# The seam between an expert loop and a linear attention: how partial sums reach one array in DRAM

## The chip, the cores and the metric

The kernel runs on one core of one Trainium2 chip. The metric is device microseconds (us) from the start to the end of one execution; lower is better. All data are float32.

The engines are named as in the profile: PE (matrix products), PEld (the loading of its weights), DVE (vector), ACT (activations), POOL (a second vector engine, which also starts indirect transfers), SP (which starts most transfers). `SPq`, `POOLq` and the like are an engine's own sequencer, which issues transfers (DMAs).

## The reference

The input has 4096 rows of 256 numbers. Four layers follow, each of the same form:

```
x = x + LN(attention(LN(x)))      # 16 heads, windows of 64 rows
x = x + LN(experts(LN(x)))        # 8 experts, each row goes to the best 2, plus a shared expert
x = x + LN(linear_attn(LN(x)))    # 16 heads, cos/sin position factors, causal, gated
x = x + LN(recurrence(LN(x)))     # forget/input/candidate gates over steps, then tanh
```

The change lies at the end of the second layer and the start of the third. The second layer is, for a row `x` (after its LN),

```
y  = sum over its 2 experts e of  weight_e * (silu(x @ w1[e]) * (x @ w3[e])) @ w2[e]     # hidden 704
y += (silu(x @ sw1) * (x @ sw3)) @ sw2                                                    # hidden 384
```

so each row of the result is a sum of three parts: two of chosen experts, one of the shared expert. The third layer needs the whole sum of a row before its LN. Its first operations are the LN of `y`, the addition to `x`, another LN, a transpose, and the products with `Wq` and `Wk`.

## The kernel before

**Units and blocks.** The 4096 rows are 32 tiles of 128 rows, or 16 *units* of 256 rows (0 to 15). For the experts, rows are sorted by expert into *blocks*: 32 large ones of 256 rows (two tiles, `nt = 2`) and 4 small ones of 128 rows (one tile). More small blocks stand in a branch (`tc.If`, L1303) that this input does not take.

**First layer (up to some 400 us).** It is written in an order fixed by hand (`ORDER_A`, `TAIL_A`), and its end sends every row to its two blocks by indirect scatters on POOL (L816), with a `memset` of the tiny tile `apart` between two of them (L964). The shared expert of units 0 to 11 is computed here (`NSA = 12`) and written to the DRAM array `ysh_d` (`shared_store`, L645); the rows of units 13 to 15 (`NSD = 13`) are set to zero (L706).

**The expert loop (400 to 890 us).** It goes over the list `line` (L1247 to 1251): the large blocks in order, and a small one after blocks 7, 15, 23 and 31. One step of the loop (for a block i)

- starts the weights of block i + 1 (`load_up`, L234 to 244, `load_down`, L246 to 260; SP),
- computes `up` of block i: in five parts of the hidden layer, each with its products (L1173), SiLU on ACT (L1178) and a product on DVE (L1180), and a rest of 64 columns,
- loads the rows of block i + 2 (`x_rows`, SP) and transposes those of block i + 1 (`x_cols`, PE and ACT),
- does one piece of a table of angles (`angle_piece`, L1071 on; DVE and ACT) and
- `down` of block i - 1: products (L1218, L1225), then for each tile a multiplication by the row's weight into a tile `yo` (DVE, L1228), and an indirect transfer that *adds* this tile to the rows of `ysh_d` (POOL, L1229).

Nobody knows at build time which rows an add touches, so the framework takes all adds to `ysh_d` as touching the same memory: each one waits until the one before it has landed. The tiles `yo` are a ring of five buffers (`tag="yo", bufs=5`).

The shared expert of unit 12 is computed at the start of the loop (`shared_part`, L1098; `shared_out`, L1126) and written to `ysh_d`. Its sums go through the same ring, as tiles `sy`.

**The seam (890 to 955 us).** After the loop, `second_weights` (L993) starts the loads of the attention's weights (`wl1`, `wl2`; SP). Then the third layer begins as a stream of small pieces: `flow(items, ORDER_C)` gives them one by one, in the order of `ORDER_C` with a lag for each piece, and `until(name, item)` issues pieces up to the first one of that name. The items are the units in the order 0, 8, 1, 9, 2, 10 ... The first pieces of a unit are

- `fy` (L322): load the unit's 256 rows of `ysh_d` into a tile `k_y` (SP); these tiles are a ring of four in the pool `kb`, which lasts to the end of the third layer,
- `bo_st`, `bo_pw`, `bo_nr`, `bo_ap` (L285 to 315): LN of `k_y` (statistics and shift on DVE, the power on POOL, the application on ACT),
- `bo_ad` (L335): add to `x` on POOL,
- `cn_st` ... `cn_ap`: the next LN, written back into `k_y`,
- `xt` (L1372, PE: four transposes `c_xt`), `xc` (L1385, ACT: copy to `c_xT`), `qk0`, `qk1` (L1391, PE: four products `c_pqk` each).

Between the pieces of units 0 and 8, PE is given the shared expert of units 13 to 15 (`shared(i, c)`, i = 0 to 2; L1322). Parts c = 0 to 2 are the three thirds of the hidden layer (`spg`: products, SiLU, product `sh` on DVE). Part 3 is the sums (`spd`: 3 products for each of two tiles; the profile shows every product as two PE instructions), copied by DVE into two tiles `sy` of the `yo` ring (L1122) and then *added* to `ysh_d` by two transfers of 128 KB on POOL, since the experts' adds have been going to those rows as well:

```
until("bo_st");  shared(0, 0..3)
until("bo_nr");  shared(1, 0)
until("bo_ad");  shared(1, 1)
until("cn_pw");  shared(1, 2);  shared(1, 3)
until("xt");     shared(2, 0..3)
```

Right behind it the loop's pools are closed, and 8 loads of 256 KB (2 MB) for the recurrence of the fourth layer are started on SP (L1354 to 1360) into the buffers of the last expert weights (`wl3`, `wl4`). The pools of the third layer (`c_sb` first, L1363) then take over the memory of the closed ones, and each new tile waits for whoever still uses that memory.

**The rest (955 to 1403 us).** The third layer continues in the order of `ORDER_C`, and the fourth layer's first steps are threaded into its end (`until("ps0", 9 + i)` and so on, L1689 on).

Of the kernel before, what the change touches and what calls it, by code (L numbers as in the profile page):

```python
# [9 lines left out]
F32 = mybir.dt.float32  # L10
I32 = mybir.dt.int32
AF = mybir.ActivationFunctionType
ALU = mybir.AluOpType
# [3 lines left out]
P = 128  # L17
D = 256
# [22 lines left out]
NSD = 13  # L41
# [99 lines left out]
def kernel(  # L141
# [7 lines left out]
    nc = tc.nc  # L149

    const = ctx.enter_context(tc.tile_pool(name="const", bufs=1))
# [114 lines left out]
    ysh_d = dram.tile([(NT + 1) * P, D], F32, name="ysh_d")  # L266
# [88 lines left out]
    row0 = const.tile([P, NB], I32, name="row0")  # L355

    key = const.tile([P, NB], F32, name="rt_key")
    n_small = const.tile([P, 1], I32, name="n_small")


# [2 lines left out]
    with ExitStack() as ph:  # L363
        wp = ph.enter_context(tc.tile_pool(name="a_w", bufs=1, side="right"))
# [253 lines left out]
        H = {}  # L618
# [62 lines left out]
        seen = pconst("rt_seen", [P, E])  # L681

        zero = wp.tile([P, XW], F32, name="zero")
        apart = wp.tile([P, 1], F32, name="apart")

        def later_constants():
            for f in range(4):
# [280 lines left out]
        with tc.manual_schedule(  # L968
# [14 lines left out]
            for it in TAIL_A:  # L983
                name, u = it.split(".")
# [8 lines left out]
    def second_weights():  # L993
# [27 lines left out]
    kb = ctx.enter_context(tc.tile_pool(name="take", bufs=2, side="right"))  # L1021
# [4 lines left out]
        out=causal, in_=causal, compare_op=ALU.is_ge, fill=0.0, base=0,  # L1026
# [6 lines left out]
        out=diag, in_=diag, compare_op=ALU.is_ge, fill=0.0, base=0,  # L1033
# [3 lines left out]
        out=diag, in_=diag, compare_op=ALU.is_ge, fill=0.0, base=31,  # L1037
# [17 lines left out]
    with ExitStack() as ph:  # L1055
        yp = ph.enter_context(tc.tile_pool(name="b_y", bufs=1, side="right"))
        hp = ph.enter_context(tc.tile_pool(name="b_h", bufs=2, side="right"))
# [40 lines left out]
        def shared_part(u, c, H):  # L1098
            xt = xnT[u // 2][:, :, (u % 2) * 256 : (u % 2) * 256 + 256]
            if c < 3:  # L1100
                pg = ps_up.tile([P, 2, BS], F32, name=f"spg{u}_{c}", tag="up")
                for i in range(2):
                    col0 = i * SHID + c * P
                    for k in range(2):
                        nc.tensor.matmul(
                            pg[:, i, :], ws_up[:, k, col0 : col0 + P], xt[:, k, :],
                            start=(k == 0), stop=(k == 1),
                        )
                sg = hp.tile([P, BS], F32, name=f"ssg{u}_{c}", tag="sg", bufs=3)
                nc.scalar.activation(sg, pg[:, 0, :], AF.Silu)  # L1110
                h = hp.tile([P, BS], F32, name=f"sh{u}_{c}", tag="h", bufs=10)
                nc.vector.tensor_tensor(h, sg, pg[:, 1, :], ALU.mult)
                H[c] = h
                return
            for t in range(2):
                pd = ps_d.tile([P, 2, D], F32, name=f"spd{u}_{t}", tag="pd")[:, 0, :]
                for i in range(3):
                    nc.tensor.matmul(
                        pd, H[i][:, t * P : (t + 1) * P], ws_down[:, i, :],
                        start=(i == 0), stop=(i == 2),  # L1120
                    )
                y = hp.tile([P, D], F32, name=f"sy{u}_{t}", tag="yo", bufs=5)  # L1122
                nc.vector.tensor_copy(y, pd)
                H[3, t] = y

        def shared_out(u, H):  # L1126
            for t in range(2):
                r0 = (2 * u + t) * P
                rows = ysh_d[r0 : r0 + P, :]
                if u < NSD:  # L1130
                    nc.sync.dma_start(out=rows, in_=H[3, t])
                else:
                    nc.gpsimd.dma_start(out=rows, in_=H[3, t], accum_op=ALU.add)


        def row_of(b):
# [6 lines left out]
        def x_rows(b, nt, at=None):  # L1143
            at = row_of(b) if at is None else at
            xg = hp.tile([P, 2, XW], F32, name=f"xg{b}", tag="xg", bufs=5)
            got = nc.sync.dma_start(
                out=xg[:, 0:nt, :],
                in_=xg_d[bass.ds(at, nt * P), :].rearrange("(t p) d -> p t d", p=P),
            )
            for name in dispatched:  # L1150
                data_dep(got, name, "a block's rows come from any token")
            return xg
# [50 lines left out]
        def down(b, nt, wb, hs, xg):  # L1203

            ws = hp.tile([P, 3, 2], F32, name=f"rt_w{b}", tag="rt_w")
            for i, op in enumerate((ALU.is_equal, ALU.not_equal)):
                nc.vector.scalar_tensor_tensor(
                    ws[:, i, 0:nt], xg[:, 0:nt, D + 2], key[:, b : b + 1], xg[:, 0:nt, D + i],
                    op, ALU.mult,
                )  # L1210
            nc.vector.tensor_tensor(ws[:, 2, 0:nt], ws[:, 0, 0:nt], ws[:, 1, 0:nt], ALU.add)
            pds = [
                ps_d.tile([P, 2, D], F32, name=f"pd{b}_{t}", tag="pd")[:, 0, :]
                for t in range(nt)
            ]
            for t in range(nt):
                for c in range(5):
                    nc.tensor.matmul(  # L1218
                        pds[t], hs[c][:, t * P : (t + 1) * P], wb[:, c, :],
                        start=(c == 0), stop=False,  # L1220
                    )

            for t in range(nt):
                r = slice(64 * t, 64 * t + 64)
                nc.tensor.matmul(pds[t], hs[5][r, :], wb[r, 5, :], start=False, stop=True)  # L1225
            for t in range(nt):
                yo = hp.tile([P, D], F32, name=f"yo{b}_{t}", tag="yo", bufs=5)
                nc.vector.tensor_scalar(yo, pds[t], ws[:, 2, t : t + 1], None, ALU.mult)  # L1228
                nc.gpsimd.indirect_dma_start(  # L1229
                    out=ysh_d[:, :],  # L1230
                    out_offset=bass.IndirectOffsetOnAxis(
                        ap=xg[:, t, D + 3 : XW].bitcast(I32), axis=0
                    ),
                    in_=yo,
                    in_offset=None,
                    compute_op=ALU.add,
                )

        def expert_of(b):
            return nc.values_load(  # L1240
                owner[0:1, b : b + 1], engines=[mybir.EngineType.SP],
                min_val=0, max_val=E - 1,
                skip_runtime_bounds_check_because="clamped where it is computed",
            )
# [2 lines left out]
        line = []  # L1247
        for i in range(NL):
            line.append((i, 2))
            if i % 8 == 7:  # L1250
                line.append((NL + i // 8, 1))
        rows = [x_rows(*line[0], 0)]

        H = {}
        for c in range(4):
            shared_part(NSA, c, H)
            next(tables, None)
        for _ in tables:
            pass
        nc.sync.dma_start(  # L1260
            out=th, in_=th_d.rearrange("f i d -> (f i d)").partition_broadcast(P)
# [8 lines left out]
        for i in range(len(line)):  # L1270
# [19 lines left out]
            if i + 1 < len(line):  # L1290
                wbs.append(load_down(i + 1, ev))
            pending = (*line[i], wbs[i], hs, rows[i])
        down(*pending)

        ws_down = shared_down(1)
# [7 lines left out]
        with tc.If(used > NS_ALWAYS):  # L1303
            for b in range(NL + NS_ALWAYS, NB):
                ev = expert_of(b)
                wa, wb = load_up(b, ev, wa_s), load_down(b, ev, wb_s)
                xg = x_rows(b, 1)
                down(b, 1, wb, up(b, 1, wa, x_cols(b, 1, xg)), xg)
# [5 lines left out]
        def until(name, item=0):  # L1314

            while todo_next[0] != (name, item):
                todo_next[0] = next(todo)

        todo_next = [next(todo)]
        H = [{}, {}, {}]  # L1320

        def shared(i, c):  # L1322
            shared_part(NSD + i, c, H[i])
            if c == 3:
                shared_out(NSD + i, H[i])
# [2 lines left out]
        until("bo_st")  # L1328
        for c in range(4):
            shared(0, c)  # L1330
        until("bo_nr")
        shared(1, 0)
        until("bo_ad")
        shared(1, 1)
        until("cn_pw")
        shared(1, 2)
        shared(1, 3)
        until("xt")
        for c in range(4):
            shared(2, c)  # L1340

    xt_stack.close()
# [9 lines left out]
    w_x = [kview(fl[:, i * 512 : (i + 1) * 512], 2) for i in range(3)]  # L1352
    w_c = [kview(fl[:, i * 512 : (i + 1) * 512], 2) for i in (3, 4)]
    w_c.append(kview(fm[:, 0:512], 2))  # L1354
    w_ox = kview(fm[:, 512:1024], 2)
    w_oc = kview(fm[:, 1024:1536], 2)
    for dst, src in zip(
        w_x + w_c + [w_ox, w_oc], (wfT, wiT, wcT, ufT, uiT, ucT, woT, uoT)
    ):
        nc.sync.dma_start(out=dst, in_=src.rearrange("(k p) f -> p k f", p=P))  # L1360

    with ExitStack() as ph:
        cb = ph.enter_context(tc.tile_pool(name="c_sb", bufs=2))  # L1363
# [315 lines left out]
        def first_cell(p):  # L1679
            f, i, g, c = (spare(8 * p + j) for j in (4, 5, 6, 7))  # L1680
            nc.vector.tensor_tensor(i, i, g, ALU.mult)
            for m in range(2):
# [2 lines left out]
                    ALU.mult, ALU.add,  # L1685
                )


        for i, u in enumerate((0, 8, 1, 9)):  # L1689
            until("ps0", 9 + i)  # L1690
# [258 lines left out]
```

## Time and profile before

| | us |
|---|---|
| median of three runs | 1393.34 |
| the three runs | 1393.34, 1394.17, 1390.73 |
| the profiled execution, its own time | 1404.6 |
| its span in the profile | 1402.9 |

The profiled execution is one execution of its own, slower than the median by 11.3 us, and every duration below is from it. Engine-busy shares are averages over the whole span: PE 95%, DVE 62%, ACT 42%, POOL 40%. The transfers move 139 MB, most of it before 910 us.

A line of the timeline has a start, a duration, the engine, the line in the kernel, the operation, "out<-in" by the program's names, the shape, and the count of like operations that follow one another. In square brackets stands how long the engine had been idle before it and what released it. Releasers are inferred: an instruction that waits for several things is put down to the one that came last by the profile, and where the one named had long been done, it was another. A line of a window gives, for a stretch of time, the busy time of each engine and the number of its instructions, then the clock granted to PE (1.00 is full speed), the busy share of the DMA engines and the rate of the transfers in GB/s.

### The profile page before, as it was taken

How to read it: one execution, taken by the hardware profiler on the slowest of the kernel's cores; microseconds unless marked ns; L12 is line 12 of the kernel's file. 1: busy time of each engine (PE TensorE's matmuls, PEld its weight loads, DVE VectorE, ACT ScalarE, POOL GpSimd, SP SyncE). 2: the span in 40 equal slices, each digit the busy share in tenths (PEclk: the TensorE clock that was granted, in tenths of full speed). 3: DMA queues.
4: the chain of work that ended last, by engine and by line, in shares of the span. 5: the costliest groups of instructions: out<-in, count | busy, mean ns of one | idle time of the engine just before them, and what ended most of it. 6: DMA issues, size and time to landing. Idle time of an engine off the chain costs nothing. (4 is left out here: it accounts for less than half of the span.)

```text
span 1402.9 us, 29800 instructions
## 1 busy us (share of the span) xinstructions
PE 1330.3 (95%) x11456; PEld 1098.0 (78%) x11456; DVE 870.2 (62%) x2586; ACT 583.2 (42%) x1306; POOL 558.3 (40%) x677
## 2 busy tenths in 40 slices
PE   6999999998699999999999999869999999999996
PEld 5888888786588888888888888646777777788885
DVE  5879787787354555555455642237878897645434
ACT  4766666563122222222222222025665665435443
POOL 3535657655311221212212212234766675433333
PEclk9999999998899999999999999979999999999998
DMA  8000111115746675666658566740000000000001
GB/s 218 2 17 21 35 44 51 47 36 195 216 145 201 174 229 162 182 202 199 197 157 233 164 204 173 137 104 22 18 18 17 18 3 2 2 1 31 16 31 45
DMA packets 120481, 139.13 MB, mean 99 GB/s; under 512 B 26704, under 2 KB 99600, under 8 KB 120336
## 3 DMA queue, kind: packets, MB, share of 16 engines
q1 hardware_dynamic: 105792, 117.91, 26.6%
q0 software_dynamic: 13728, 18.23, 6.9%
q8 instruction: 92, 1.51, 0.4%
q10 hardware_dynamic: 816, 1.06, 0.2%
q14 instruction: 53, 0.43, 0.1%
HBM read 104.83 MB, written 32.33 MB: 98 GB/s over the span
## 5 line engine op out<-in xcount | busy, mean ns | idle before, releaser
L1173 PE MATMUL pg<-xgT,wa 128*128 128x256 f32 (+1 forms) x1440 | 305.5, 371 | 1.8 <-ACT xgT L1162 1.8
L1173 PEld LDWEIGHTS pg<-xgT,wa 128*128 128x128 f32 x1440 | 259.9, 191 | 45.8 <-issue 11.3
L1229 POOL DMA_INDIRECT ysh_d<-yo,xg x68 | 106.2, 1562 | 427.3 <-DVE yo L1228 211.7
L1178 ACT ACTIVATE sg<-pg 128x256 f32<-128x256 f32 (+1 forms) x180 | 66.9, 372 | 354.6 <-PE pg L1173 353.6
L1180 DVE TENSOR_TENSOR h<-sg,pg 128x256 f32<-128x256 f32 (+1 forms) x180 | 73.0, 406 | 204.3 <-ACT sg L1178 201.7
L1218 PE MATMUL pd<-wb,h 128*128 128x256 f32 x680 | 152.8, 379 | 0.0
L1218 PEld LDWEIGHTS pd<-wb,h 128*128 128x128 f32 x680 | 126.4, 190 | 16.0 <-issue 0.3
L523 POOL TENSOR_TENSOR a_pn<-a_p,a_ri 128x512 f32<-128x512 f32 x64 | 66.6, 1045 | 90.1 <-DVE a_ri L517 50.2
L1527 DVE TENSOR_TENSOR c_et<-c_pe,causal 128x512 f32<-128x512 f32 x128 | 83.2, 682 | 22.2 <-PE c_pe L1517 21.9
L816 POOL DMA_INDIRECT xg_d<-xrow,slot x64 | 64.8, 1012 | 23.0 <-issue 9.9
L632 PE MATMUL a_sh<-xnT,was 128*128 128x256 f32 x288 | 73.4, 401 | 0.0
L1391 PE MATMUL c_pqk<-wl,c_xT 128*128 128x512 f32 x128 | 63.8, 622 | 8.0 <-ACT c_xT L1385 7.9
L1781 PE MATMUL d_pg<-d_xT,wl 128*128 128x256 f32 x288 | 70.2, 379 | 0.0
L632 PEld LDWEIGHTS a_sh<-xnT,was 128*128 128x128 f32 x288 | 56.2, 199 | 8.8
L1781 PEld LDWEIGHTS d_pg<-d_xT,wl 128*128 128x128 f32 x288 | 54.6, 190 | 7.6 <-ACT d_gt L1787 0.2
L496 DVE TENSOR_REDUCE a_mx<-a_s 128x8 f32<-128x512 f32 x64 | 42.7, 683 | 16.7 <-PE a_s L486 16.1
L1461 POOL TENSOR_TENSOR c_kn<-c_sq,xrow 128x512 f32<-128x512 f32 x32 | 42.2, 1319 | 12.9 <-ACT c_sq L1404 12.9
L1391 PEld LDWEIGHTS c_pqk<-wl,c_xT 128*128 128x128 f32 x128 | 23.2, 193 | 27.0 <-issue 16.1
L502 DVE TENSOR_TENSOR a_p<-a_s,a_mx 128x512 f32<-128x512 f32 x64 | 43.2, 675 | 0.8
L510 ACT ACTIVATE a_p<-a_p 128x512 f32<-128x512 f32 x64 | 40.1, 629 | 7.3 <-DVE a_p L502 6.7
L515 DVE TENSOR_REDUCE a_sm<-a_p 128x8 f32<-128x512 f32 x64 | 43.1, 674 | 0.0
L1082 DVE SCALAR_TENSOR_TENSOR ang<-kk,ang 128x256 f32<-128x256 f32 x96 | 40.9, 426 | 3.3
(313 smaller groups left out, 2787.0 us busy)
## 6 DMA issues: line engine op xcount, KB each, us to landing
wa<-in_w_dram SPq DMA_DIRECT2D x36, 704.0 KB
wa<-in_w_dram SPq DMA_DIRECT2D x36, 640.0 KB
wb<-in_w_dram SPq DMA_DIRECT2D x36, 640.0 KB
xg<-xg_d SPq DMA_DIRECT2D x32, 260.0 KB
xg_d<-zero SPq DMA_DIRECT2D x8, 650.0 KB
wb<-in_w_dram SPq DMA_DIRECT2D x72, 64.0 KB
x<-in_x_dram SPq DMA_DIRECT2D x16, 256.0 KB
k_y<-ysh_d SPq DMA_DIRECT2D x16, 256.0 KB
```

Source lines behind the costliest of these rows:

```text
L502: nc.vector.tensor_tensor(pr, S[u]["s"][g], S[u].pop(("m", g)).unsqueeze(2).to_broadcast([P, 8, 64]), ALU.subtract,)
L523: nc.gpsimd.tensor_tensor(to, S[u].pop(("p", g)), S[u].pop(("ri", g)).unsqueeze(2).to_broadcast([P, 8, 64]), ALU.mult,)
L632: nc.tensor.matmul(to[:, i, :], ws_up[:, k, col0 : col0 + P], turned(b)[:, k, :], start=(k == 0), stop=(k == 1),)
L816: dma = nc.gpsimd.indirect_dma_start(out=xg_d[:, :], out_offset=bass.IndirectOffsetOnAxis(ap=slots[i][:, t : t + 1], axis=0), in_=sent[:, ...
L1173: nc.tensor.matmul(pg[:, i, 0:n], wa[:, k, col0 : col0 + P], xt[:, k, 0:n], start=(k == 0), stop=(k == 1),)
L1178: nc.scalar.activation(sg[:, 0:n], pg[:, 0, 0:n], AF.Silu)
L1180: nc.vector.tensor_tensor(h[:, 0:n], sg[:, 0:n], pg[:, 1, 0:n], ALU.mult)
L1218: nc.tensor.matmul(pds[t], hs[c][:, t * P : (t + 1) * P], wb[:, c, :], start=(c == 0), stop=False,)
L1229: nc.gpsimd.indirect_dma_start(out=ysh_d[:, :], out_offset=bass.IndirectOffsetOnAxis(ap=xg[:, t, D + 3 : XW].bitcast(I32), axis=0), in_=yo ...
L1391: nc.tensor.matmul(pq[:, 0:n], S2[u]["xT"][:, k, t * P : (t + 1) * P], w[:, k, :], start=(k == 0), stop=(k == 1),)
L1527: nc.vector.tensor_tensor(masked, S2[u]["pe", t][i], causal.unsqueeze(1).to_broadcast([P, 4, P]), ALU.mult,)
L1781: nc.tensor.matmul(pg[:, m, :], a, r, start=(i == 0), stop=(i == len(prods) - 1))
```

## The change

It has six edits, numbered for later reference.

1. **Adds side by side.** The two adds of a large block are declared independent of each other (`declare_no_dep`, a group `add{b}` for each block): a row can be in a block only once, so the two tiles touch different rows. Adds of different blocks still wait for each other. A `memset` of `apart` (now a tile that lasts, from the constants' pool) is put on POOL ahead of each add.
2. **Small blocks forward.** The four small blocks come after blocks 3, 11, 19 and 27 instead of 7, 15, 23 and 31. The last block of the loop is then a large one.
3. **Sums of the shared expert in a lasting ring.** Units 12 to 15 put both their tiles into one tile `k_sh` of the `k_y` ring (four buffers, shared with the loaded units) instead of two tiles of the `yo` ring, and write or add it with one transfer of 256 KB instead of two of 128 KB.
4. **The `yo` ring** has four buffers instead of five.
5. **Parts of the shared expert moved.** Unit 14's first two parts come directly behind unit 13's, ahead of `bo_nr`; part 2 follows `bo_nr`, part 3 follows `bo_ad`, and unit 15's first part stands ahead of `xt`.
6. **Recurrence weights later.** The 8 loads are issued in the third layer, when its stream has reached item 6's `fy`, instead of at the seam.

```diff
+    apart = const.tile([P, 1], F32, name="apart")
...
-        apart = wp.tile([P, 1], F32, name="apart")
...
-                y = hp.tile([P, D], F32, name=f"sy{u}_{t}", tag="yo", bufs=5)
-                nc.vector.tensor_copy(y, pd)
-                H[3, t] = y
+                if t == 0:
+                    H[3] = kb.tile([P, 2, D], F32, name=f"k_sh{u}", tag="k_y", bufs=4)
+                nc.vector.tensor_copy(H[3][:, t, :], pd)
 
         def shared_out(u, H):
-            for t in range(2):
-                r0 = (2 * u + t) * P
-                rows = ysh_d[r0 : r0 + P, :]
-                if u < NSD:
-                    nc.sync.dma_start(out=rows, in_=H[3, t])
-                else:
-                    nc.gpsimd.dma_start(out=rows, in_=H[3, t], accum_op=ALU.add)
+            rows = ysh_d[u * 256 : (u + 1) * 256, :].rearrange("(t p) d -> p t d", p=P)
+            if u < NSD:
+                nc.sync.dma_start(out=rows, in_=H[3])
+            else:
+                nc.gpsimd.dma_start(out=rows, in_=H[3], accum_op=ALU.add)
...
             for t in range(nt):
-                yo = hp.tile([P, D], F32, name=f"yo{b}_{t}", tag="yo", bufs=5)
+                yo = hp.tile([P, D], F32, name=f"yo{b}_{t}", tag="yo", bufs=4)
                 nc.vector.tensor_scalar(yo, pds[t], ws[:, 2, t : t + 1], None, ALU.mult)
-                nc.gpsimd.indirect_dma_start(
+
+                nc.gpsimd.memset(apart, 0.0)
+                dma = nc.gpsimd.indirect_dma_start(
                     out=ysh_d[:, :],
...
+                tc.declare_no_dep(dma.ins, group=f"add{b}", reason="an expert has a token once")
+                tc.add_to_no_dep_group(f"add{b}", dma.ins)
...
-            if i % 8 == 7:
+            if i % 8 == 3:
                 line.append((NL + i // 8, 1))
...
         for c in range(4):
             shared(0, c)
+        shared(1, 0)
+        shared(1, 1)
         until("bo_nr")
-        shared(1, 0)
+        shared(1, 2)
         until("bo_ad")
-        shared(1, 1)
+        shared(1, 3)
         until("cn_pw")
-        shared(1, 2)
-        shared(1, 3)
+        shared(2, 0)
         until("xt")
-        for c in range(4):
+        for c in range(1, 4):
             shared(2, c)
...
-    for dst, src in zip(
-        w_x + w_c + [w_ox, w_oc], (wfT, wiT, wcT, ufT, uiT, ucT, woT, uoT)
-    ):
-        nc.sync.dma_start(out=dst, in_=src.rearrange("(k p) f -> p k f", p=P))
+    def last_weights():
+        for dst, src in zip(
+            w_x + w_c + [w_ox, w_oc], (wfT, wiT, wcT, ufT, uiT, ucT, woT, uoT)
+        ):
+            nc.sync.dma_start(out=dst, in_=src.rearrange("(k p) f -> p k f", p=P))
...
+        until("fy", 6)
+        last_weights()
 
         for i, u in enumerate((0, 8, 1, 9)):
```

## The prediction

> **What bounds the kernel now.** The profiled execution took 1404.6 us (span 1402.9), the three runs had a median of 1393.34 us. First I read the page's busy table and slices, then three stretches with their busy time (columns: stretch, length, busy PE, PEld, DVE, ACT, POOL, then PE clock, DMA share, GB/s).
>
> ```profile
> PE 1330.3 (95%) x11456; PEld 1098.0 (78%) x11456; DVE 870.2 (62%) x2586; ACT 583.2 (42%) x1306; POOL 558.3 (40%) x677
> PE   6999999998699999999999999869999999999996
> ```
> ```profile
> 400.00:890.00 490.00, 490.00 (x2416) 415.78 (x2415) 252.70 (x743) 114.78 (x305) 101.53 (x65) 1.00 0.65 188
> 890.00:955.00 65.00, 46.12 (x190) 31.24 (x188) 20.86 (x65) 15.38 (x34) 24.27 (x26) 0.87 0.50 104
> 955.00:1360.00 405.00, 401.15 (x5034) 315.82 (x5035) 283.86 (x792) 215.77 (x476) 217.29 (x265) 1.00 0.05 15
> ```
>
> The expert loop and the linear attention keep PE busy without a gap, so an edit counts there only if it touches PE. Between them, at the second seam, PE idles 18.9 us of 65 and runs part of the rest at half clock. I took that stretch in order of time. PE:
>
> ```profile
> 901.54 5.34 PE L1105 MATMUL spg<-xnT,was 128*128 128x256 f32 x24
> 912.67 1.22 PE L1118 MATMUL spd<-wbs,sh 128*128 128x256 f32 x2 [5.79 <-DVE sh L1112]
> ...
> 928.50 0.60 PE L1376 MATMUL c_xt<-ident,k_y 128*128 128x128 f32 x4
> 937.03 3.78 PE L1391 MATMUL c_pqk<-wl,c_xT 128*128 128x512 f32 x4 [7.93 <-ACT c_xT L1385]
> ...
> 944.26 0.33 PE L1376 MATMUL c_xt<-ident,k_y 128*128 128x128 f32 x1 [0.74 <-ACT k_y L313]
> ```
>
> Two waits, 5.79 and 7.93 us, make most of it. Behind the first, on POOL and DVE:
>
> ```profile
> 880.06 1.55 POOL L1229 DMA_INDIRECT ysh_d<-yo,xg  x1 [5.82 <-DVE yo L1228]
> 886.27 1.55 POOL L1229 DMA_INDIRECT ysh_d<-yo,xg  x1 [4.66 <-DVE rt_w L1211]
> 890.73 1.55 POOL L1229 DMA_INDIRECT ysh_d<-yo,xg  x1 [2.90 <-DVE rt_w L1211]
> 895.36 1.55 POOL L1229 DMA_INDIRECT ysh_d<-yo,xg  x1 [3.08 <-DMA ysh_d<-yo,xg]
> 901.64 1.55 POOL L1229 DMA_INDIRECT ysh_d<-yo,xg  x1 [4.73 <-issue]
> ```
> ```profile
> 908.11 0.76 DVE L1123 COPY sy<-spd 128x256 f32<-128x256 f32 x2 [8.45 <-DMA ysh_d<-yo,xg]
> 910.92 0.43 DVE L292 BATCH_NORM_STATS2 st_bo<-k_y 128x6 f32<-128x256 f32 x1 [2.06 <-DMA k_y<-ysh_d]
> ```
>
> The last five adds (blocks 30, 31 and the small one) go one after another: each starts when the last has landed, 6.2, 4.5, 4.6, 6.3 and 6.4 us apart, the last landing at 908.0. Only then may DVE copy unit 13's sums (their buffers are those of `yo`) and SP load the first unit, which lands at 910.92. Behind the second, on ACT and SP:
>
> ```profile
> 936.39 0.59 ACT L1385 COPY c_xT<-c_xt 128x512 f32<-128x512 f32 x1 [10.23 <-DMA k_y<-ysh_d]
> ```
> ```profile
> 903.21 0.43 SPq L1011 DMA_DIRECT2D wl<-in_bo_dram  x1
> ...
> 908.03 0.89 SPq L324 DMA_DIRECT2D k_y<-ysh_d  x2
> 925.71 0.37 SPq L1360 DMA_DIRECT2D wl<-in_wfT_dram  x1
> ```
>
> The profile names a `k_y` load, but the copy does not read it. `c_xT` is the first tile of a pool that takes over the memory of `yo`, so in the built program it waits for all adds from that memory; the last, unit 15's, was issued on POOL at 929.42 and lands under 2 MB of recurrence weights, at about 936.3.
>
> **The change, part by part.**
>
> *Adds side by side, small blocks forward.* One landing a block instead of two. The last block is now a large one: PE still ends at 892.3, block 30's down products one block's 5.1 us (4.48 + 0.70, overlapped) before, at 887.2. Its first add follows 0.8 later as at 880.06: 888.0. The second stands 1.55 + 0.12 (the memset `apart` between two scatters in the routing) + 0.2 behind: 889.9. It lands 4.5 later (few loads are then in flight): 894.4. The last block's pair: 894.5 and 896.4; with the attention weights in flight 6.1 us to land: 902.5. Landing times seen here run from 4.4 to 7.8 (661.69 to 669.51 in the loop), so 900.8 to 905.9. SP has its last weight load out at 903.6, so the first unit's load goes at 903.7, not 908.03. The windows show the weights' traffic until 907.3; the 256 KB stand behind it, about 1 us: landed at 908.3, against 910.92. Ends: 906.6 (2.9 us as before) and 909.6 (lands late, then 2.9 + queue). I take 908.3, nearest to the rows of that traffic.
>
> 68 or so memsets of 0.11 us with gaps of 0.2 cost nothing: POOL is busy 102 of 490 us in the loop. With four buffers instead of five, a buffer comes back two blocks (30 us) later, against 1.9 + 7.8 us for an add: nothing. Small blocks four large blocks earlier in each eight: PE's sum is the same, and PE had no wait beside them after blocks 7, 15 and 23; nothing.
>
> *Sums in the `k_y` ring.* Unit 13's copies go when their products are done (902), so `sh14_0` and `sh14_1` are no longer stuck behind them. The third, `sh14_2`, stands behind the first unit's statistics: 908.3 + 1.45 (910.92 to the fifth operation's end) + 0.42 = 910.2. PE meanwhile ends the up products at 907.3 (0.45 later than before, because DVE copies two tiles before the branch) and four of the down products at 908.2: it waits 2.0 us instead of 5.79 + 1.30 + 0.39. Then 8 products (0.22 each) to 912.0 and unit 15's 24 to 917.4, before 925.7.
>
> What is late next: POOL must issue unit 14's add (256 KB, rows of 128 KB: 0.9 each, so 0.9 to 1.8) ahead of the residual adds, and that waits for the copies at 912.6. Residual adds 913.6 to 915.0, statistics 2.4 after their start, 916.0, power 0.8, shift, ACT's two applications 1.1: 918.1; two activations and `sh15_2`: 919.3. PE waits 1.9 us here. Eight products and the transposes: 921.7. `c_xT` now waits for adds of blocks only, landed at 902.5: it runs at 921.75, and `c_pqk` at 922.35 instead of 937.03: 14.7 us.
>
> The copies of unit 15 wait for unit 13's add: issued at 904, landed by 912 at 7.8: hidden by 9 us.
>
> *Clock.* PE's row fell to 0.50 at 910.5, 3.6 us after PE stopped, and again at 934. Without such a stop the first four `c_pqk` take 1.98, as the next four did, instead of 3.78. The next wait is unit 8's: copies at 921.7, ACT to 923.4, POOL's add of unit 15 and residual adds 923.0 to 924.4, statistics 925.4, power 926.1, `c_sq` until 927.2, so the second `c_xt` at 927.8 instead of 944.26: 16.4. After that the order on PE is the same; I give back 0.4 for the waits of 0.91 and 0.31 behind it, which may grow at full clock. Sum 16.0.
>
> Clock rule, in sentences of their own: The Trainium skill, "TensorE: Matmul & The Clock Gate", Part 1, says the clock halves after an idle window of about 3.4 us and needs as long to come back, with free-running windows. The 3.6 us agree. By it a stop of 2.0 us costs no clock; if the first unit landed at the upper end, the stop would be 3.3 and could, and the sum would be 14 instead of 16.
>
> *Weights later.* SP no longer waits 16.7 us for PE (925.71) before units 1 and 9. Unit 1's load now waits for unit 14's add instead (its buffer): issued 912.6, landed by 920.4 at 7.8, load 2.9: 923.3, needed at 926.1. Units 1 and 9 load before the weights, which go at about 930 and are first read after 1290: nothing.
>
> DMA rule: the Trainium skill's "DMA: Bandwidth & Descriptors", Anatomy of one DMA, fits 2.0 us + bytes/436e3, an estimate of 2.3 us for a 128 KB add. The rows say 4.4 to 7.8, so the measurement decides; by that fit unit 15's add would have landed at 931.7, and the second wait would give about 10, not 14.7.
>
> **Sum.** 1404.6 - 16.0 = 1388.6 in the profiled execution's own time. The median lies 11.3 us lower, and nothing shows where. Taken as spread evenly it leaves the gain: 1393.3 - 15.9, about 1377.5; I say 1378.
>
> **Rivals.**
> - *Unit 1 late.* If unit 14's add of 256 KB takes twice the 7.0 us of the slowest 128 KB one (929.42 to 936.4), it lands at 926.6, unit 1 at 929.5, 3.4 us late: 1381. Against: that one had 2 MB beside it, this one nothing.
> - *The runs without a profile lose less at the seam.* If the 11.3 us sit in the seam's landings, 4.7 us remain to gain: 1388.6. For: the excess is unexplained. Against: the seam has five landings of hundreds of transfers.
> - *No change*: `c_xT` still waits for a late landing: 1393. Against: the sums now lie in a pool that outlives this one.
> - *Slower: pairs delay weights in the loop.* PE has no wait there, and wins nothing there. Two adds at once beside the loads (share 0.65) could make a block's weights late. 16 us over 36 blocks: from 0.44 us a block on it is slower; at 0.7 us it gives 1378 + 25 = 1403. Against: weights issued at 404.7 to 405.9 are read at 417.4, 11.5 us for 1.4 MB, 122 GB/s where 188 flow.
>
> **Chances.** Forecast 0.55, unit 1 late 0.14, seam cheaper without profile 0.13, no change 0.07, slower 0.11. A difference under 0.3% (4.2 us) can't be told from none. Faster 0.55 + 0.14 + 0.13 = 0.82, same 0.07, slower 0.11. Range: below, all 18.9 us of idle and 3 of half clock gone would be 1371.5, say 1372; above, 1389 takes in the third case; no change and slower, 0.18, stay out.
>
> **What would show it.** The loop's PE row still at 490 of 490; POOL's adds in pairs 1.9 us apart; `st_bo` at 908 to 909; the wait at `spd` under 3 us and no half clock before 920; `c_pqk` 14 to 15 us earlier with no wait on ACT; PE idle in the seam about 6 us in place of 18.9. It is wrong if `c_pqk` or the second `c_xt` waits for something I have as landed, or if PE waits in the loop.

## The result, and the profile after

The changed kernel takes 1381.64 us (median of four runs, 1380.4 to 1383.21) against 1392.1 for the kernel before in the same comparison. The ratio is 0.9917, with a 95% interval from 0.9905 to 0.9929. The forecast was 1378 from 1393.3, so two thirds to three quarters of the forecast gain of 15.9 us came: 10.5 by the medians, 11.6 by the ratio.

Three stretches of the profile after (columns: stretch, length, busy PE, PEld, DVE, ACT, POOL, then PE clock, DMA share, GB/s):

```profile
400.00:890.00 490.00, 488.41 (x2404) 413.57 (x2403) 248.82 (x734) 114.09 (x304) 111.34 (x131) 1.00 0.64 186
890.00:955.00 65.00, 55.50 (x496) 39.22 (x495) 33.70 (x92) 26.31 (x58) 26.62 (x28) 0.95 0.41 97
955.00:1360.00 405.00, 400.47 (x4790) 318.36 (x4789) 278.32 (x779) 210.91 (x464) 215.45 (x264) 1.00 0.05 15
```

The loop is as it was: the 1.6 us of idle in the first row are the branch (1.12, which now falls into this stretch) and one wait of 0.38 for weights. The second row is where the gain is: PE idles 9.5 us of 65 instead of 18.9. The forecast had about 6. Where the rest stayed is seen in the order of time, first on PE:

```profile
884.66 5.42 PE L1105 MATMUL spg<-xnT,was 128*128 128x256 f32 x24 [1.12 <-DVEq L1305]
889.92 3.09 PE L1118 MATMUL spd<-wbs,sh 128*128 128x256 f32 x12
892.84 5.34 PE L1105 MATMUL spg<-xnT,was 128*128 128x256 f32 x24
898.02 1.03 PE L1118 MATMUL spd<-wbs,sh 128*128 128x256 f32 x4
904.20 3.78 PE L1118 MATMUL spd<-wbs,sh 128*128 128x256 f32 x8 [5.15 <-DVE sh L1112]
...
918.76 1.98 PE L1395 MATMUL c_pqk<-wl,c_xT 128*128 128x512 f32 x4 [0.68 <-ACT c_xT L1389]
```

The first line is unit 13's first product, at 884.66 here and 893.36 before. From here on times are counted from this line (written "+"), because what lies ahead of it differs between executions. The first `c_pqk` is at +34.10; it was at +43.67. The wait of 7.93 us for `c_xT` is gone (0.68 is left). The wait ahead of the second `spd` line is not: 5.15 us instead of 5.79 + 1.30 + 0.39. Its cause, on POOL, SP and DVE of the kernel after:

```profile
879.19 1.57 POOL L1229 DMA_INDIRECT ysh_d<-yo,xg  x1 [11.08 <-DVE yo L1226]
...
881.07 1.57 POOL L1229 DMA_INDIRECT ysh_d<-yo,xg  x1 [0.19 <-issue]
...
885.63 1.57 POOL L1229 DMA_INDIRECT ysh_d<-yo,xg  x1 [2.88 <-issue]
...
887.51 1.57 POOL L1229 DMA_INDIRECT ysh_d<-yo,xg  x1 [0.19 <-POOLq L1305]
893.77 1.28 POOL L1131 DMA_DIRECT2D ysh_d<-k_sh  x1 [4.69 <-DVE k_sh L1124]
```
```profile
894.15 0.43 SPq L1011 DMA_DIRECT2D wl<-in_bo_dram  x1
894.70 0.89 SPq L324 DMA_DIRECT2D k_y<-ysh_d  x2
```
```profile
902.44 0.43 DVE L292 BATCH_NORM_STATS2 st_bo<-k_y 128x6 f32<-128x256 f32 x1 [5.11 <-DMA k_y<-ysh_d]
```

The adds go in pairs 1.9 us apart, and the last one is issued at +2.85 instead of +8.28. But the first unit's load is issued behind the last attention weight (+10.04), and its statistics start at +17.78, 7.7 us after its issue, on landing; before, it was issued at +14.67 and there at +17.56. Earlier adds brought no earlier first unit.

### The profile page after: what moved, and what is told of

Read it like the earlier page. It is cut to its first block, busy times and chain, and to the rows that moved or that the text cites. A ratio compares the mean times of both kernels' runs of the same rounds, so it can differ in the third digit from the quotient of the medians.

```text
span 1381.5 us, 29860 instructions
## 1 busy us (share of the span) xinstructions
PE 1319.3 (95%) x11456; PEld 1092.6 (79%) x11456; DVE 873.5 (63%) x2586; ACT 583.1 (42%) x1306; POOL 564.9 (41%) x742
## 5 line engine op out<-in xcount | busy, mean ns | idle before, releaser
L1171 PEld LDWEIGHTS pg<-xgT,wa 128*128 128x128 f32 x1440 | 260.4, 191 | 47.5 <-issue 11.3
L1228 POOL MEMSET apart<- 128x1 f32 x68 | 47.9, 704 | 0.0
L1797 POOL TENSOR_TENSOR d_gt<-d_gt,d_gt 128x512 f32<-128x512 f32 x14 | 18.8, 1342 | 60.5 <-ACT d_gt L1793 58.9
```

The source lines that it names most:

```text
L1171: nc.tensor.matmul(pg[:, i, 0:n], wa[:, k, col0 : col0 + P], xt[:, k, 0:n], start=(k == 0), stop=(k == 1),)
L1228: nc.gpsimd.memset(apart, 0.0)
```

## The experiments

Each kernel was compared with the kernel before on the same chip; the ratios are compared below, not the times, because the last four ran where the kernel before takes 1404.35 us, the others where it takes 1392.1 to 1393.5. "Unit 1" is the start of the third unit's transposes, from where both kernels run without a long wait; it is counted from unit 13's first product in one profile each.

| kernel | ratio to before, 95% interval | first unit's load issued | its statistics | first `c_pqk` | unit 1 |
|---|---|---|---|---|---|
| before, first profile | | +14.67 | +17.56 | +43.67 | +63.15 |
| before again (`e_before`) | | +13.70 | +16.61 | +42.31 | +61.51 |
| after | 0.9917 [0.9905, 0.9929] | +10.04 | +17.78 | +34.10 | +51.79 |
| `u_pairs` | 0.9925 [0.9911, 0.9939] | +14.99 | +17.72 | +34.03 | +51.72 |
| `n_all` | 0.9888 [0.9873, 0.9903] | +6.65 | +12.59 | +28.01 | +45.70 |
| `n_hold` | 0.9898 [0.9880, 0.9915] | +9.23 | +15.42 | +31.50 | +49.20 |
| `n_allp` | 0.9939 [0.9926, 0.9953] | +12.49 | +15.17 | +36.18 | +53.87 |
| `n_two` | 0.9890 [0.9875, 0.9906] | +6.64 | +12.58 | +27.22 | +44.92 |
| `o_ring` | 0.9978 [0.9967, 0.9988] | +11.64 | +16.87 | +36.60 | +57.09 |
| `u_ring` | 0.9969 [0.9957, 0.9981] | +9.62 | +16.60 | +36.45 | +56.87 |
| `u_late` | 0.9952 [0.9937, 0.9966] | +9.35 | +16.63 | +32.94 | +55.04 |
| `u_order` | 0.9937 [0.9925, 0.9950] | +9.95 | +17.05 | +36.27 | +53.97 |
| `u_small` | 0.9921 [0.9908, 0.9934] | +10.89 | +17.11 | +33.41 | +51.10 |
| `o_adds` | 1.0005 [0.9996, 1.0014] | +9.63 | +16.25 | +42.61 | +62.50 |

A difference of 0.001 in the ratio is 1.4 us.

### Where the first profile's extra time lay

`e_before` is the kernel before, unchanged.

> The kernel before, unchanged, for a second profile of it. If the 11.3 us by which its first profiled execution exceeded the median lie ahead of the expert loop, this profile has the loop's first transposes about 11 us earlier than 372.59, at 361 to 363, and the seam as it was: from the first spg of unit 13 to the second c_xt 50.9 us, the loop before it (first transposes to spg) 520.8 us, a span near 1391. If instead they lie in the seam's landings, the first transposes stay near 372 and the seam shrinks to about 40 us.

It took 1393.25 us, with a span of 1391.5. The loop's first transposes, in its timeline on PE, and the same line of the first profile of before:

```profile
361.50 1.11 PE L1158 MATMUL xgt<-ident,xg 128*128 128x128 f32 x4 [9.59 <-DMA xg<-xg_d]
```
```profile
372.59 1.11 PE L1158 MATMUL xgt<-ident,xg 128*128 128x128 f32 x4 [8.54 <-DMA xg<-xg_d]
```

They stand 11.1 us apart, nearly all of the 11.4 us between the two spans. So the extra time lay ahead of the expert loop, and the seam is the same but for 1.6 us (+63.15 and +61.51). The last four kernels, on the chip where everything takes 12 us more, also have this line at 370.8 to 372.7; the other profiles have it at 360.4 to 361.6. That the first profile came from such a chip is likely, not shown.

### The adds, the attention weights, and what stands in the first unit's way

Theory A says that the first unit is late because its load stands behind the attention weights, theory B that the adds make it late.

`u_pairs`, the adds of a block waiting for each other again:

```diff
-                tc.declare_no_dep(dma.ins, group=f"add{b}", reason="an expert has a token once")
-                tc.add_to_no_dep_group(f"add{b}", dma.ins)
```

> The changed kernel with the two adds of a block waiting for each other again (small blocks still forward). Adds at the end go at 879.2, 883.7, 888.2 and 892.7 (4.5 apart) in place of 879.2, 881.1, 885.6, 887.5, and the last lands at about 898 instead of some 894.5. Theory A, the first unit's load is late because the attention weights stand in front of it in the queue: their traffic lasts to about 900 anyway, so the load lands at 902.5 to 904 instead of 902.4 and the time is 1381.6 plus 0 to 2 us. Theory B, the load is late because of the adds: it moves with them, 3.5 to 4 us later, and with the clock the time is 1386 to 1388.

The ratio rose by 0.0008, which the two intervals do not tell from nothing. The last adds, the load and the statistics, in the timelines of POOL, SP and DVE of `u_pairs` (unit 13's first product is at 882.80):

```profile
887.44 1.57 POOL L1229 DMA_INDIRECT ysh_d<-yo,xg  x1 [2.98 <-DVE sh L1112]
...
891.97 1.57 POOL L1229 DMA_INDIRECT ysh_d<-yo,xg  x1 [2.84 <-DVE k_sh L1124]
```
```profile
892.58 0.44 SPq L1011 DMA_DIRECT2D wl<-in_bo_dram  x1
897.79 25.94 SPq L324 DMA_DIRECT2D k_y<-ysh_d  x6
```
```profile
900.52 0.43 DVE L292 BATCH_NORM_STATS2 st_bo<-k_y 128x6 f32<-128x256 f32 x1 [5.05 <-DMA k_y<-ysh_d]
```

The last add goes 6.3 us later than in the changed kernel and the load 4.95 us later (+14.99), but now the load needs 2.7 us instead of 7.7, and the unit is there at the same moment. What the adds won, the load lost in the queue. Theory A.

`n_all`, the first unit's load ahead of all attention weights on SP:

```diff
-        wl, wm, kview = second_weights()
         until("bo_st")
+        wl, wm, kview = second_weights()
```

> The changed kernel with the first unit's load of ysh_d put ahead of all loads of attention weights on SP, which then follow it. Theory A: the load goes when the last add has landed, at 892 to 894, and lands 2.6 to 3.5 us later, at 895 to 897, before PE wants the third part of unit 14 (898.9); PE's stop of 5.15 us and the half clock behind it (2 us) go, the second wait of 1.39 stays or grows by up to 2: 1381.6 - 5 to - 7, so 1375 to 1377. The weights land by 906, and the first c_pqk, at about 912, does not wait for them. Theory B: the load still lands at 900 or later because adds are in flight; the time stays within 1.5 us of 1381.6.

It took 1377.13 us, ratio 0.9888, 4 us below the changed kernel. Its timeline on SP, DVE and PE (first product at 883.09):

```profile
889.74 0.37 SPq L324 DMA_DIRECT2D k_y<-ysh_d  x1
890.28 2.27 SPq L1002 DMA_DIRECT2D wl<-in_wq_dram  x2
```
```profile
895.34 0.42 DVE L1112 TENSOR_TENSOR sh<-ssg,spg 128x256 f32<-128x256 f32 x1 [1.30 <-ACT ssg L1110]
895.68 0.42 DVE L292 BATCH_NORM_STATS2 st_bo<-k_y 128x6 f32<-128x256 f32 x1
```
```profile
896.45 3.09 PE L1118 MATMUL spd<-wbs,sh 128*128 128x256 f32 x12
899.38 5.34 PE L1105 MATMUL spg<-xnT,was 128*128 128x256 f32 x24
904.55 0.59 PE L1118 MATMUL spd<-wbs,sh 128*128 128x256 f32 x2
907.56 2.42 PE L1118 MATMUL spd<-wbs,sh 128*128 128x256 f32 x10 [2.41 <-DVE sh L1112]
...
911.10 1.98 PE L1395 MATMUL c_pqk<-wl,c_xT 128*128 128x512 f32 x4 [0.67 <-ACT c_xT L1389]
```

The load goes at +6.65, which also shows that the last add, issued at +2.81, has landed by then; DVE finds the rows there without a wait, and all 12 `spd` products run in one piece. The stop of 5.15 us is gone, and the clock stays at 1.00 through the seam. The first `c_pqk` is at +28.0, where the prediction had it (+29.0).

`n_hold`, the add of unit 13's sums held back behind the first unit's power on POOL:

```diff
-            if c == 3:
+            if c == 3 and i:
                 shared_out(NSD + i, H[i])
...
         until("bo_nr")
+        shared_out(NSD, H[0])
```

> The changed kernel with the add of unit 13's sums (256 KB, issued at 893.77, 0.9 us ahead of the first unit's load) held back on POOL until behind the first unit's power, so that it goes at about 904. Theory A: the load still stands behind the weights; it gains at most the share of the add's 256 KB, 0 to 1 us, and the copy of unit 15 does not wait for the add (904 + 5 is before 916): 1380.5 to 1382. Theory B: without the add the load takes 3 us instead of 7.7: landed at 898, PE's stop under 1 us, the time 1375 to 1377.

1378.99 us, ratio 0.9898: 2.6 us below the changed kernel by the medians, between the two expectations; the two intervals overlap, so the step is not clear of noise. The load took 6.2 us, and the unit was there 2.4 us earlier than in the changed kernel's profile. Not all of that is shown to be the add's: in `u_small`, `u_late` and `u_order`, which have the add in place, the load takes 6.2 to 7.3 us and the unit is there at +16.6 to +17.1, still 1.2 to 1.7 us later than here. So the 256 KB add that goes 0.9 us ahead of the load is a small part of what it stands behind, 1.2 to 2.4 us; the weights are more. Theory A had 0 to 1 us for it.

`n_allp` is `n_all` with the edit of `u_pairs`.

> The changed kernel with the first unit's load ahead of the attention weights, as in n_all, but with the two adds of a block waiting for each other again, as in u_pairs. Counted from unit 13's first product: the last add goes at 9.2 instead of 2.8, the first unit's load at about 14.5 instead of 6.7, it lands at 17.3, PE stops for some 5 us again, and the weights, now behind it, land by 27, before the first c_pqk at 34. Theory A (side by side adds are worth something only where the load goes as soon as they have landed): 1381.5 to 1384, so 4.5 to 6 us above n_all's 1377.1, where the same edit undone in the changed kernel cost 1.0. Rival C (n_all gained because the weights no longer compete with the adds and sums): about 1377 to 1379.

Ratio 0.9939, so 0.0051 (7 us) above `n_all`: the same edit that is worth nothing in the changed kernel is worth 7 us once the load can go as soon as the adds have landed. On PE (first product at 883.42):

```profile
900.34 3.20 PE L1118 MATMUL spd<-wbs,sh 128*128 128x256 f32 x8 [2.53 <-DVE sh L1112]
...
914.37 4.11 PE L1118 MATMUL spd<-wbs,sh 128*128 128x256 f32 x10 [4.75 <-DVE sh L1112]
```

The wait for the first unit came back (2.53 us where some 5 were expected, with half clock behind it), and a second one of 4.75 us with it, which was not expected: the second unit's load now stands behind weights that start 6 us later, and DVE takes unit 15's `sh` only behind that unit's statistics. The median of 1384.66 lies 0.7 above theory A's range and far from rival C's. Rival C falls.

`n_two`, the first two units' loads ahead of the weights:

```diff
-        wl, wm, kview = second_weights()
         until("bo_st")
...
         until("xt")
+        wl, wm, kview = second_weights()
```

> The changed kernel with the loads of the first two units (0 and 8) ahead of all attention weights on SP. In n_all the second unit's load stood behind the weights (issued at 16.9 after unit 13's first product, landed at 22.7), and DVE ran unit 15's last product only behind it: PE waited 2.41 us there. With the load landed by 12, this wait falls to 0.5 to 1.5 us, the rest of the order stays: 1375.5 to 1376.5 against 1377.1. If the wait has another cause (ACT's two applications of the first unit), it stays at 2.4 and the time at 1377.

The wait for unit 15's last part fell from 2.41 to 1.63 us, where 0.5 to 1.5 were expected, and unit 1 came 0.8 earlier in the profile. The time did not follow: 1377.48 us misses the expected 1375.5 to 1376.5, and the ratio of 0.9890 is not told apart from `n_all`'s 0.9888. By the ratios both are some 4 us below the changed kernel; the interval of `n_all` ends at 0.9903, where that of the changed kernel begins at 0.9905, and that of `n_two` at 0.9906.

### The sums in the lasting ring

`o_ring` is the kernel before with only this part (one tile `k_sh` a unit in the `k_y` ring, one transfer), `u_ring` the changed kernel without it. `u_ring` also has five `yo` buffers again; their number was not tried by itself. The edit of `o_ring`, which `u_ring` turns round:

```diff
-                y = hp.tile([P, D], F32, name=f"sy{u}_{t}", tag="yo", bufs=5)
-                nc.vector.tensor_copy(y, pd)
-                H[3, t] = y
+                if t == 0:
+                    H[3] = kb.tile([P, 2, D], F32, name=f"k_sh{u}", tag="k_y", bufs=4)
+                nc.vector.tensor_copy(H[3][:, t, :], pd)
...
```

> The kernel before with one part of the change alone: the shared expert's sums in the k_y ring, with one transfer a unit. Theory A (the gain is the end of c_xT's wait for the last add, of 8 us, and of DVE's wait for the adds): the first unit still lands at 17.6 after unit 13's first product, as in both kernels, so the seam is nearly that of the changed kernel: 1383 to 1386. Rival D (the adds, small blocks, order and later weights carry an equal part): 1387 to 1390.

> The changed kernel with the sums back in the yo ring (five buffers) and two transfers a unit; all other parts stay. Theory A: c_xT again waits for the landing of unit 15's add, issued at about 33.7 after unit 13's first product and landed 4 to 6 us later (no recurrence weights beside it): the first c_pqk at 38 to 40 instead of 34.1, some half clock behind the wait, 1386 to 1389. Rival D: 1382 to 1384.

Alone, it brought 0.0022 (3 us); taken away, it cost 0.0052 (7 us). PE's timeline of `o_ring` and of `u_ring`:

```profile
918.98 1.98 PE L1389 MATMUL c_pqk<-wl,c_xT 128*128 128x512 f32 x4 [0.68 <-ACT c_xT L1383]
...
928.13 1.09 PE L1482 MATMUL c_tq<-ident,c_qr 128*128 128x128 f32 x4 [2.69 <-DVE c_qr L1459]
929.01 2.81 PE L1389 MATMUL c_pqk<-wl,c_xT 128*128 128x512 f32 x4
```
```profile
919.54 3.78 PE L1397 MATMUL c_pqk<-wl,c_xT 128*128 128x512 f32 x4 [4.72 <-ACT c_xT L1391]
```

The mechanism is as predicted: with the sums in the old ring `c_xT` waits (4.72 us, and the four products behind it take 3.78 instead of 1.98), with them in the lasting ring it does not. But alone the part does not hold its gain. With the recurrence weights still at the seam, PE stops 9 us later at `c_tq` for 2.69 us, with half clock behind it. The runs of `o_ring` spread from 1385.8 to 1391.2, and its profile, taken at 1385.84, is the fastest of them, so what cost the slower ones was not seen. The median of 1390.34 misses expectation A (1383 to 1386) and lies just above D's upper end of 1390. The profile shows one stop by which the part alone falls short; the 4.5 us between the profiled execution and the median stay open. `u_ring`, at 1388.44, came out as theory A had it.

### The later weights, the order, the small blocks

`u_late`, the recurrence weights at the seam again:

```diff
+    last_weights()
...
-        until("fy", 6)
-        last_weights()
```

> The changed kernel with the recurrence weights loaded at the seam again; all other parts stay. The prediction's account (the later weights cost and gain nothing): 1381 to 1382.5. Rival E (SP waits for PE's last product of unit 15 before the first of these loads, 28.7 after unit 13's first product, and the third unit's load, which went at 28.6, now stands behind 2 MB: issued at 33.5, landed at 41 instead of 32; DVE, whose statistics of that unit stand ahead of the angles' products, and then PE wait for it, as in o_ring, where PE waited 2.69 us there and had half clock behind it): 1385 to 1387.

Ratio 0.9952, 0.0035 above the changed kernel: 4.9 us, as rival E had it. SP, DVE and PE of `u_late` (first product at 892.84):

```profile
921.34 0.37 SPq L1364 DMA_DIRECT2D wl<-in_wfT_dram  x1
...
925.62 0.47 SPq L1364 DMA_DIRECT2D wl<-in_uoT_dram  x1
926.20 35.90 SPq L324 DMA_DIRECT2D k_y<-ysh_d  x6
```
```profile
933.09 0.43 DVE L292 BATCH_NORM_STATS2 st_bo<-k_y 128x6 f32<-128x256 f32 x1 [2.96 <-DMA k_y<-ysh_d]
```
```profile
935.20 1.09 PE L1490 MATMUL c_tq<-ident,c_qr 128*128 128x128 f32 x4 [2.96 <-DVE c_qr L1467]
```

The third unit's load is issued at +33.36 behind the 2 MB. DVE waits 2.96 us for it, and the angles' products `c_qr`, which stand behind its statistics on DVE, make PE wait as long. Unit 1 is 3.3 us later than in the changed kernel.

`u_order`, unit 14's and 15's parts among the first unit's pieces as before:

```diff
-        shared(1, 0)
-        shared(1, 1)
         until("bo_nr")
-        shared(1, 2)
+        shared(1, 0)
         until("bo_ad")
-        shared(1, 3)
+        shared(1, 1)
         until("cn_pw")
-        shared(2, 0)
+        shared(1, 2)
+        shared(1, 3)
         until("xt")
-        for c in range(1, 4):
+        for c in range(4):
```

> The changed kernel with the parts of units 13 to 15 in the old order among the first unit's pieces. The first unit still lands at 17.7 after unit 13's first product, and now all three parts of unit 14 stand behind its statistics on DVE, so PE waits three times (about 5, 1.3 and 0.4 us, as in the kernel before and in o_ring) instead of once, with unit 15's parts closing up behind: the first c_pqk at 36.6 instead of 34.1. 1383.5 to 1385. If the order is worth nothing because PE only waits for the same landing, 1381 to 1382.5.

Ratio 0.9937, 0.0020 (2.8 us) above the changed kernel, with intervals that just overlap (from 0.9925 here, to 0.9929 there); the first `c_pqk` is at +36.27. PE waits 5.29, 1.31 and 0.39 us for unit 14's parts, one after another, as in the kernel before.

`u_small`, the small blocks back behind blocks 7, 15, 23 and 31 (`if i % 8 == 7`), and `o_adds`, the kernel before with the pairs side by side and the small blocks forward:

> The changed kernel with the small blocks back behind blocks 7, 15, 23 and 31. The last add is then the small block's single one, issued when the pair of block 31 has landed, at 0 to 2 after unit 13's first product, landed by 9; the first unit's load stands behind the attention weights on SP until about 10 anyway. Theory A: no change, 1381 to 1382.5. If the prediction's step holds (one landing fewer brings the first unit earlier): the load goes 3 to 4 us later, 1384 to 1386.

> The kernel before with the adds of a block side by side and the small blocks forward, and nothing else. Theory A: the last add lands 5 us earlier, but the first unit's load stands behind the attention weights and lands at 17.6 after unit 13's first product as before, and c_xT waits for unit 15's add as before: 1391.5 to 1393.5, no change. The prediction's account (each landing saved brings the first unit 2.6 us earlier): 1389 to 1390.5.

`u_small`: 0.0004 above the changed kernel, no difference; `o_adds`: 1.0005, no difference, although its last add goes at +2.68 instead of +8.0 to +8.3 and its first unit's load at +9.63 instead of +13.7 to +14.7. The unit is there at +16.25, against +16.61 and +17.56 in the two profiles of the kernel before.

## Why the prediction was right or wrong

**Right: the bound, the sign and the main mechanism.** The gain lies in the seam: of the 10.0 us between the spans of `e_before` and the changed kernel, 9.7 lie between unit 13's first product and unit 1. Of the rest, 1.2 came behind unit 1, unexplained, and the loop took 0.9 more. `c_xT` no longer waits for unit 15's add: 0.68 us in place of 7.93. The loop did not get shorter: 523.09 us from the first transposes to unit 13's first product, against 520.77 and 522.24 in the two profiles of before and 520.57 to 522.44 in the rest. The last four adds were put at 888.0, 889.9, 894.5 and 896.4; 8.70 us earlier, by the shift of unit 13's first product, that is 879.3, 881.2, 885.8 and 887.7, and they went at 879.19, 881.07, 885.63 and 887.51. The load's issue was put at 903.7, which shifts to 895.0; it went at 894.70.

**Wrong: "the 256 KB stand behind it, about 1 us: landed at 908.3".** This is the step that failed. The load landed 7.7 us after its issue, not 4.6; in the prediction's time at about 911, beyond its upper end of 909.6. In the queue ahead of it were the attention weights, whose last loads landed later than estimated (the last one 5.9 us after its issue, at about +15.4), and unit 13's add, which the step did not count (`n_hold`: 1.2 to 2.4 us). The Trainium skill, "DMA: Bandwidth & Descriptors", "Queues, rings and completion order", says that on each DMA engine the descriptors of SP's transfers are consumed in the order in which they stand in the ring. That agrees with 7.7 us behind the weights in the changed kernel and 2.7 us in `u_pairs`, whose load goes at a moment when the windows of 1 us show no transfer at all (DMA share 0.00 from +15.0 to +16.0).

**What followed from it.** The stop at `spd` was put at 2.0 us, without loss of clock; it was 5.15 and the clock fell to 0.50. The eight products behind it took 3.57 us (904.20 to 907.77) instead of 8 × 0.22 = 1.76. The two, 3.15 + 1.8, are nearly the 5.1 us by which the first `c_pqk` (+29.0 predicted, +34.10 measured) and the second `c_xt` (+34.4 predicted, 924.19 - 884.66 = +39.53 measured) came late. So the sum was 16.4 - 5.1 = 11.3 against the first profile of before (944.26 - 893.36 = +50.90), which is 11.4 when measured. The seam of the second profile of before is shorter, its second `c_xt` at +49.26, and against that one the gain is 9.7. With the load ahead of the weights, in `n_all`, the second `c_xt` is at +33.44, 1 us ahead of the predicted +34.4, and the ratio of 0.9888 is a gain of 15.6 us, where 15.9 were forecast: the step that failed is worth about what was missing.

**Wrong: side by side adds as the source of the earlier first unit.** The step "one landing a block instead of two" was right on POOL and won nothing: undone, it cost nothing that can be measured (`u_pairs`), the small blocks likewise (`u_small`), and the two without the rest brought nothing (`o_adds`). It pays 7 us only with the load ahead of the weights (`n_all` against `n_allp`).

**Wrong: "Weights later ... nothing".** Undone, this part costs 4.9 us. The prediction saw that SP no longer waits 16.7 us ahead of the third unit's load, but left out that this wait comes into play once the longer ones are gone: at an earlier seam, 2 MB ahead of the third unit's load make it late. The sum had the third unit on time, so the step's price stood in the 16 us without being told.

**The order** was not priced by itself; undone, it costs 2.8 us. Undone one by one, the ring, the weights and the order cost 7, 5 and 3 us, together more than the whole gain: what one of them wins is in part lost without another.

**The rivals.** The third unit was not late in the changed kernel (no wait of PE for it). The extra 11.3 us of the first profile did not lie in the seam, but for 1.6, so that rival fell, and with it the doubt about the comparison. "No change" and "pairs delay weights in the loop" fell with the rows above: one wait of 0.38 us for weights in the loop.

**The clock.** The prediction read the first fall of the clock as 3.6 us after PE's stop; in finer windows it lies at 910.04, 3.2 us after. In every trace whose clock changes in the seam, the moments of change lie whole multiples of 3.41 us apart (in `n_allp` at 900.97, 904.38, 914.62 and 918.04; from a change at 368.50 to the first of these it is 156 times 3.4133). So it looks as if the clock is decided at the end of each window of that length, by how much PE did in it. Three such windows of `n_allp` and two of `n_all`; the second number is PE's busy time:

```profile
897.56:900.97 3.41, 0.88 (x5) 0.58 (x4) 1.75 (x7) 0.00 (x0) 0.88 (x2) 1.00 1.07 155
907.80:911.21 3.41, 1.83 (x9) 1.27 (x7) 0.50 (x3) 1.63 (x4) 0.72 (x1) 1.00 1.04 214
911.21:914.62 3.41, 0.25 (x1) 0.25 (x2) 1.90 (x7) 0.00 (x0) 0.54 (x1) 1.00 0.38 118
```
```profile
902.89:906.30 3.41, 2.26 (x11) 1.65 (x9) 1.76 (x8) 1.39 (x4) 0.77 (x2) 1.00 0.83 173
906.30:909.71 3.41, 2.15 (x10) 1.91 (x11) 1.89 (x7) 0.24 (x1) 0.69 (x1) 1.00 0.26 78
```

The first and the third are followed by a granted clock of 0.50, the others are not. In the seams of all traces, a window at full clock was followed by half clock when PE had been busy for at most 1.36 us of it (`o_adds`, 925.88 to 929.29), and never when it had been busy for 1.83 us or more. So the stop of 2.53 us in `n_allp` and the one of 2.78 us in `n_hold` lost the clock. The one of 2.41 us in `n_all` (905.15 to 907.56) did not, and that was luck: the last change of its clock ahead of the loop is at 367.00, and 158 times 3.4133 us later, at 906.30, an edge cuts the stop in two. The prediction weighed the rule of the Trainium skill, "TensorE: Matmul & The Clock Gate", Part 1: half clock after an idle window of about 3.4 us, the windows free-running. The traces agree with the length and the free running, but not with a window that must be idle throughout: a fall of the clock came with PE busy for a quarter of it (0.88 of 3.41 us).

## What to carry to other kernels

An earlier producer is worth nothing while the consumer's load stands in a queue behind something else: before pricing a shorter chain of writes, look at what its reader's load is queued behind, in issue order and in bytes in flight, and put the load that the next engine waits for ahead of the loads that are needed 20 us later. Waits that lie behind one another hide each other's price: undoing one part of a change, with the others in place, shows what it is worth there, and doing it alone can show something else, here 7 us against 3.

## What the runs showed that was not expected

The same edit, adds side by side, measured 0 in the changed kernel and 7 us in one that differs from it only in the place of one call. And stops of PE of 2.5 and 2.8 us were enough to lose the clock, while one of 2.4 us kept it because of where it fell.
